# A planner that takes the results of TensorE to be visible later after the end of a step

## Chip, cores and metric

The kernel runs on one core of a Trainium2 chip. The metric is the device time of one execution in microseconds (us). Time before: 4647.31 us, the median of three runs (4646.46 to 4648.82).

## The reference, cut to what matters

The input x holds 32 images of 96 channels and 56 x 56 pixels in f32. Two layers follow each other.

```python
# layer 0: inverted bottleneck, 96 -> 576 -> 96
h = relu(bn(einsum('oc,bchw->bohw', w1, x)))
h = relu(bn(depthwise3x3(h, wdw)))
x = x + bn(einsum('oc,bchw->bohw', w2, h))
# layer 1: tokens t (32, 3136, 96)
t = to_tokens(x)
h = relu(bn(ln(t) @ w1.T))                       # 96 -> 192
X = fft(h, axis=1, norm='ortho')                 # over the 3136 tokens
xr = relu(X.real * rd - X.imag * id + rb)
xi = relu(X.imag * rd + X.real * id + ib)
t = t + bn(ifft(xr + 1j * xi).real @ w2.T)       # 192 -> 96
t = t + ffn(ln(t))      # 96 -> 384 -> 96, operands rounded to fp8 (5,2), sums to f16
```

## The kernel before, in words

Each image passes through four groups of steps, and several images are under way at once.

- **Units** (`unit`, 8 an image: two strips of 28 rows times four blocks of 128 hidden channels). TensorE (PE) expands 96 channels to 128 (L615), ScalarE (ACT) evicts the PSUM result with bias and relu (L625), and the depthwise 3x3 taps are shared out: one on ACT into `acc` (L641), one or two on ACT into `product` (L657), which the GpSimd queue adds to `acc` by an accumulating DMA (L676), and the other six or seven on VectorE (DVE, L668). ACT ends with a relu (L685). The last 64 channels (`last_channels`) go through PE alone (L717, L753), evicted by ACT (L736, L740, L782).
- **front** (one a strip, with `mixer_in`, two a strip). PE projects the hidden channels back in a chain of seven steps (L881, L897, L915) in the PSUM tile `pw`; ACT evicts (L928); DVE takes the layer norm (L825 to L854, with a root on ACT, L835) and scales (L974). PE transposes (L982), projects to 192 (L1000), and does the first stage of the Fourier transform (L1031); ACT evicts each (L985, L1013, L1037). The result goes through DRAM.
- **mid** (two an image). PE does the second Fourier stage (L1118), ACT and DVE apply the diagonal weights and the relus (L1130 to L1165), PE projects 192 to 96 (L1204, L1216; eviction L1230) and inverts the first stage (L1243 to L1247; eviction L1258). Again through DRAM.
- **back** (four an image). PE finishes the inverse (L1324), DVE adds it to the residual (L1329) and takes the norm; ACT quantizes (L1345); PE transposes (L1357; eviction L1361) and computes the feed-forward layer (L1378, L1423) with ACT and DVE in between (L1390, L1396, L1405, L1432, L1435); PE sums up (L1442, L1453), ACT evicts (L1458) and SyncE stores. For the last three images the quantizing goes to DVE.

**What sets the order.** No instruction's place is written by hand. The code above only registers *steps* with the class `Plan`: each has an engine, a planned cost in us, the steps that it comes after, the buffers that it takes at its start and gives back at its end, and a rank. `Plan.emit` then plays the program through once in planned time, while the program is being built: whenever an engine is idle it takes the ready step of the lowest rank whose buffers are free, emits its instructions, and counts the engine as busy for the planned cost. The order in which steps are taken becomes the order of each engine's queue. [...]the planned times have no further effect.

A step's followers become ready, and its buffers free, not at its planned end but a time `late` after it: `Plan.LATE` gives this for PE, ACT and DVE, 0.1 us for the others, and transfers have a rule of their own (`moved`). It applies to every follower, so also to a PE step that comes after another PE step. For PE there are two more rules. [...] And where PE has nothing ready although steps are left,[...] the planner emits a *filler* (L1486), a matmul whose result is not used, to keep the clock up, and counts it as 0.23 us.

Buffers that PE shares with others: three PSUM pairs of banks (`ps`), taken by nearly every PE step or chain and given back by the ACT or DVE step that reads the result; `pw`, one; the SBUF tiles `hs` (3), `acc` (7), `z` (2), `V` (2), `eo` (3), `xnT`, `ya`, `xt`, `u8`, `uT`, `h8` (1 each) and others. A PE step cost is planned by `pe(n, m, passes)`, an ACT step by `act`, a DVE step by `dve`:

```python
def pe(n, m, passes):
    return passes * max(0.855 * n, 0.88 * m) / 1000
```

The line numbers in the profile are those of the program below.

Of the kernel before, what the change touches and what calls it, by code (L numbers as in the profile page):

```python
# [153 lines left out]
class Plan:  # L154
# [5 lines left out]

    LATE = {"PE": 0.23, "ACT": 0.18, "DVE": 0.15}
    WINDOW = 3.413
    LITTLE, FULL = 0.58, 0.965

# [46 lines left out]
    def step(self, engine, cost, emit, after=(), take=(), give=(), late=None, rank=None):  # L213
        late = self.LATE.get(engine, 0.1) if late is None else late
        if rank is None:
            rank = self.now
            self.now += self.pace
        s = Step(engine, cost, emit, list(after), list(take), list(give), late, rank, len(self.steps))
        self.steps.append(s)
        return s  # L220
# [1333 lines left out]
```

## Time and profile before

The span of the profiled execution is 4642.4 us, its mean granted TensorE clock 0.994 of full speed.

| stretch, us | PE busy | DVE busy | ACT busy | granted clock |
|---|---|---|---|---|
| 0 to 150 | 118.20 | 113.23 | 73.72 | 0.85 |
| 150 to 600 | 426.07 | 424.50 | 360.30 | 0.98 to 1.00 |
| 600 to 4200 (3600) | 3537.34 | 3449.78 | 3369.36 | 1.00 |
| 4200 to 4500 (300) | 287.51 | 249.82 | 246.12 | 0.99 to 1.00 |
| 4500 to 4642 | 126.92 | 97.96 | 71.67 | 1.00 |

Two things help in reading the profile of this kernel. Busy time of PE counts matmuls whose ends are modelled, each 0.16 us beyond the start of the next one in a dense stream, so short holes between PE steps don't show as idle time. And a line of the waits names an instruction, the one that released it, the total idle time of the engine just before such instructions, how often, and the longest; it is a wait at the head of a queue[...].

The largest groups are the taps on DVE (L668: 1664 of 1793 ns, 2972.6 us), the expansion (L615) and the projection (L881) on PE (805.3 and 792.8 us), and the product on ACT (L657: 384 of 1588 ns, 609.4 us).

### The profile page before, as it was taken

How to read it: one execution, taken by the hardware profiler on the slowest of the kernel's cores; microseconds unless marked ns; L12 is line 12 of the kernel's file. 1: busy time of each engine (PE TensorE's matmuls, PEld its weight loads, DVE VectorE, ACT ScalarE, POOL GpSimd, SP SyncE). 2: the span in 40 equal slices, each digit the busy share in tenths (PEclk: the TensorE clock that was granted, in tenths of full speed). 3: DMA queues.
4: the chain of work that ended last, by engine and by line, in shares of the span. 5: the costliest groups of instructions: out<-in, count | busy, mean ns of one | idle time of the engine just before them, and what ended most of it. 6: DMA issues, size and time to landing. Idle time of an engine off the chain costs nothing.

```text
span 4642.4 us, 89413 instructions
## 1 busy us (share of the span) xinstructions
PE 4496.0 (97%) x35608; PEld 3351.9 (72%) x35608; DVE 4335.3 (93%) x7053; ACT 4121.2 (89%) x5390; POOL 339.9 (7%) x397
## 2 busy tenths in 40 slices
PE   7999999999999999999999999999999999999998
PEld 4667777777777777777777777777777777777777
DVE  7899999999999999999999999999999999999956
ACT  4677999999999999999999999999999999999854
POOL 0100000000000000000000000000000000000000
PEclk8999999999999999999999999999999999999999
DMA  3577877767877777777767877767776867877753
GB/s 78 130 160 174 192 168 179 183 166 181 187 170 171 187 168 179 185 174 171 184 165 181 187 169 171 187 167 180 187 172 171 187 165 179 191 170 171 170 148 100
DMA packets 390902, 789.51 MB, mean 170 GB/s; under 512 B 135600, under 2 KB 236532, under 8 KB 390484
## 3 DMA queue, kind: packets, MB, share of 16 engines
q1 hardware_dynamic: 335028, 479.15, 37.0%
q0 software_dynamic: 55296, 304.64, 34.1%
q8 instruction: 280, 4.59, 0.4%
q14 instruction: 138, 1.13, 0.1%
q10 hardware_dynamic: 160, 0.01, 0.0%
HBM read 286.38 MB, written 192.68 MB: 103 GB/s over the span
## 4 chain that ended last, share of the span: by engine, by line
PE 56%; ACT 14%; DVE 14%; DMA 5%; issue 3%; SPq 0%; DVEq 0%; ACTq 0%; POOLq 0%
PE pw L881 14%; PE ps L615 9%; DVE acc L668 7%; PE ps L1118 4%; PE ps L1031 3%; PE ps L1000 3%; PE ps L1324 3%; ACT product L657 3%; DMA acc<-product 3%; PE ps L1216 2%; PE ps L753 2%; PE ps L1378 2%; PE pw L915 2%; PE ps L1423 2%; PE ps L717 1%
## 5 line engine op out<-in xcount | busy, mean ns | idle before, releaser
L668 DVE SCALAR_TENSOR_TENSOR acc<-hs,wdw,acc 128x1540 f32<-128x1540 f32 (+2 forms) x1664 | 2972.6, 1793 | 30.1 <-ACT acc L641 22.1
L615 PE MATMUL ps<-xs,w1T 96*128 96x406 f32 x2048 | 805.3, 515 | 18.7 <-ACT hs L625 13.7
L881 PEld LDWEIGHTS pw<-w2T,acc 128*112 128x112 f32 x7168 | 749.4, 178 | 63.6 <-issue 44.5
L881 PE MATMUL pw<-w2T,acc 128*112 128x96 f32 x7168 | 792.8, 264 | 0.5 <-ACT acc L685 0.5
L657 ACT ACTIVATE product<-hs,wdw 128x1568 f32<-128x1568 f32 (+1 forms) x384 | 609.4, 1588 | 17.8 <-DMA product<-product 17.4
L625 ACT ACTIVATE hs<-ps,b 128x812 f32<-128x812 f32 x512 | 478.7, 935 | 114.9 <-PE ps L615 85.1
L615 PEld LDWEIGHTS ps<-xs,w1T 96*128 96x128 f32 x2048 | 363.1, 191 | 251.2 <-issue 177.4
L676 POOL DMA_DIRECT2D acc<-product x256 | 224.6, 877 | 3317.1 <-DVE rf L854 936.7
L641 ACT ACTIVATE acc<-hs,bd,wdw 128x1568 f32<-128x1568 f32 x256 | 435.4, 1701 | 0.2
L685 ACT ACTIVATE acc<-acc 128x1568 f32<-128x1568 f32 x256 | 387.5, 1514 | 42.8 <-DMA acc<-product 42.6
L753 PE MATMUL ps<-hl,band 128*64 128x385 f32 (+3 forms) x3072 | 416.0, 495 | 0.2 <-ACT gc L1258 0.2
L1000 PE MATMUL ps<-watt,xnT 97*120 97x192 f32 x1792 | 334.1, 330 | 16.7 <-DVE V L1147 13.4
L1000 PEld LDWEIGHTS ps<-watt,xnT 97*120 97x120 f32 x1792 | 292.5, 183 | 71.9 <-issue 35.8
L1118 PEld LDWEIGHTS ps<-wb,yb 112*128 112x128 f32 x3528 | 296.6, 165 | 52.2 <-issue 16.0
L1390 ACT ACTIVATE h<-ps 128x784 f16<-128x784 f32 x384 | 315.5, 824 | 15.4 <-PE ps L1378 10.1
L1405 ACT ACTIVATE h<-h 128x784 fp8e5<-128x784 f16 x348 | 298.8, 859 | 34.0 <-DVE h L1396 33.7
L1118 PE MATMUL ps<-wb,yb 112*128 112x112 f32 x3528 | 321.2, 270 | 5.8 <-ACT h L1390 2.5
L1345 ACT ACTIVATE u<-tt,mf,rf 112x96 fp8e5<-112x96 f32 x812 | 315.2, 463 | 0.6 <-DVE mf L857 0.6
L753 PEld LDWEIGHTS ps<-hl,band 128*64 128x64 f32 (+1 forms) x3072 | 152.2, 134 | 209.9 <-issue 180.0
L1486 PE MATMUL pw<-ident 128*128 128x128 f32 x1862 | 268.2, 283 | 3.4 <-ACT xt L928 3.4
L1486 PEld LDWEIGHTS pw<-ident 128*128 128x128 f32 x1862 | 247.4, 197 | 24.9 <-issue 12.5
L1396 DVE TENSOR_SCALAR h<-h,b1q 128x784 f16<-128x784 f16 x384 | 160.2, 418 | 83.9 <-ACT h L1390 81.9
(170 smaller groups left out, 6788.0 us busy)
## 6 DMA issues: line engine op xcount, KB each, us to landing
acc<-product POOLq DMA_DIRECT2D x256, 784.0 KB, 7.3
product<-product POOLq DMA_DIRECT2D x128, 756.0 KB, 10.6
yb<-ydr SPq DMA_DIRECT2D x252, 294.0 KB
wd<-in_wd_dram SPq DMA_DIRECT2D x128, 349.1 KB
wb<-in_wb_dram SPq DMA_DIRECT2D x63, 686.0 KB
ydr<-ya SPq DMA_DIRECT2D x256, 168.0 KB
xs<-in_x_dram SPq DMA_DIRECT2D x64, 609.0 KB
tdr<-xt SPq DMA_DIRECT2D x64, 588.0 KB
```

What stands on the lines that cost most here:

```text
L615: nc.tensor.matmul(u[h][:, j, 0:QW], lhsT=w1T[:, 128 * k : 128 * (k + 1)], rhs=xs[img, s][0:C, at : at + QW], start=True, stop=True,)
L625: nc.scalar.activation(flat[:, 2 * h * QW : 2 * (h + 1) * QW].rearrange("p (j w) -> p j w", j=2), u[h][:, :, 0:QW], AF.Relu, bias=b1[:, k ...
L641: nc.scalar.activation(acc[img, s, k], u["hs"][:, o + up : o + up + R, :], AF.Identity, scale=weight(up, 0), bias=bd[:, k : k + 1],)
L657: nc.scalar.activation(u["p", dr][:, ra:rb, :], u["hs"][:, ra + o + dr : rb + o + dr, :], AF.Copy, scale=weight(dr, 0))
L668: nc.vector.scalar_tensor_tensor(dst, src, weight(dr, dc), dst, ALU.mult, ALU.add)
L685: nc.scalar.activation(acc[img, s, k], acc[img, s, k], AF.Relu)
L753: nc.tensor.matmul(pv[:, :, ca:cb], lhsT=band[rows, j, dc + 1, 64 * o : 64 * o + 64], rhs=H[rows, q : q + 7, ca + dc : cb + dc], skip_grou ...
L881: nc.tensor.matmul(u["pw"][0:SK, t, n % 4, 0:C], lhsT=src[rows, (G * t + n) * SK : (G * t + n + 1) * SK], rhs=rhs, skip_group_check=True, **k,
L1000: nc.tensor.matmul(pv[0:PK, q - a, 0:HA], lhsT=xnT[:, q, 0:PK], rhs=watt, start=True, stop=True,)
L1118: nc.tensor.matmul(o, lhsT=lhsT, rhs=u["wb"][:, G * s + q, :], start=True, stop=True)
L1390: nc.scalar.activation(u["h", c].rearrange("p (j w) -> p j w", j=2), u["H", c][:, :, 0:n], AF.Copy)
L1486: nc.tensor.matmul(pw[:, 0, 4 * C :], lhsT=ident, rhs=ident, start=False, stop=False, skip_group_check=True)
```

## The change

One constant of the planner: the time after the planned end of a PE step at which its followers count as ready and its buffers as free.

```diff
-    LATE = {"PE": 0.23, "ACT": 0.18, "DVE": 0.15}
+    LATE = {"PE": 0.4, "ACT": 0.18, "DVE": 0.15}
```

It is meant to keep ACT and DVE from standing at the head of their queues for a PE result that isn't there yet: in planned time a consumer that becomes ready later finds its engine already given to other ready work, and so it is queued behind that. The arithmetic, the tiles, the buffers and the costs are those of before.

## The prediction

> **What bounds the kernel now.** I read the page first. Its first part gives busy time by engine:
>
> ```profile
> PE 4496.0 (97%) x35608; PEld 3351.9 (72%) x35608; DVE 4335.3 (93%) x7053; ACT 4121.2 (89%) x5390; POOL 339.9 (7%) x397
> ```
>
> Three engines are nearly full at once. Then I took the busy time by stretches, three of them in the middle, each about one image long (columns: stretch, length, busy time of PE, PEld, DVE, ACT, POOL, granted clock, DMA share, GB/s):
>
> ```profile
> 1200.00:1338.50 138.50, 135.64 (x1088) 100.95 (x1086) 132.41 (x211) 129.65 (x172) 11.34 (x13) 1.00 0.74 175
> 1338.50:1477.00 138.50, 136.34 (x1088) 100.86 (x1087) 132.99 (x217) 129.39 (x174) 9.10 (x11) 1.00 0.74 179
> 1477.00:1615.50 138.50, 135.61 (x1083) 100.53 (x1081) 132.25 (x207) 129.36 (x172) 11.96 (x14) 1.00 0.74 173
> ```
>
> Between 600 and 4200 us L668 ran 1347 times; at 52 a image (1664 over 32) that is 25.9 images, so 139 us an image. Of these PE is busy for 136, DVE for 132.5, ACT for 129.5. No engine bounds alone: what the total hangs on is how well one order fits three streams, and 32 x 139 = 4448 us of the 4647 lie in this repetition. The same stretches for the filler line alone show that the order repeats every two images, to the instruction (one filler is two records):
>
> ```profile
> 1200.00:1339.00 139.00, 6.45 (x44) 5.74 (x44) 1.00 0.74 175
> 1339.00:1478.00 139.00, 3.94 (x24) 3.51 (x24) 1.00 0.74 179
> 1478.00:1617.00 139.00, 6.45 (x44) 5.74 (x44) 1.00 0.74 174
> 1617.00:1756.00 139.00, 3.94 (x24) 3.50 (x24) 1.00 0.75 180
> ```
>
> So the planner has settled into a cycle. A changed constant makes it settle into another, and whatever that costs or saves is paid some 30 times. Next, who waits, in the waits between 600 and 4200 us, first DVE's, then ACT's, then PE's (total, times, longest):
>
> ```profile
> DVE tt L1329 <- PE ps L1324: 52.7, 82, 1.7
> DVE h L1396 <- ACT h L1390: 47.3, 42, 2.9
> ACT hs L625 <- PE ps L615: 43.3, 104, 0.8
> ACT al L782 <- PE ps L753: 36.3, 29, 1.3
> ACT z L1013 <- PE ps L1000: 19.6, 24, 1.2
> ACT y L1432 <- PE ps L1423: 16.6, 16, 1.7
> PE ps L1442 <- DVE V L1147: 13.0, 24, 0.9
> PE ps L1423 <- ACT xnT L985: 11.7, 11, 1.1
> ```
>
> Waits on PE cost DVE 52.7/26 = 2.0 us an image; all of ACT's added up are 164 us, 6.3 an image; PE's own are 62.7 us, 2.4 an image. Last, what LATE claims against what the trace has, in the timeline (start, length, engine, line, idle time before):
>
> ```profile
> 2036.47 1.63 PE L615 MATMUL ps<-xs,w1T 96*128 96x406 f32 x4 [0.24 <-ACT h L1390]
> 2037.94 0.73 PE L1246 MATMUL ps<-pj,wc 112*112 112x336 f32 x2
> 2038.14 0.94 ACT L625 ACTIVATE hs<-ps,b 128x812 f32<-128x812 f32 x1 [0.18 <-PE ps L615]
> ```
>
> PE was free for its next step at 2037.94; ACT, which had been idle, started on the result at 2038.14, 0.20 us later. The planner's cost for this step is 4 x 0.855 x 406 = 1.39 us; from 2036.47 to 2038.14 are 1.67, so counted from the planned end the result was late by 0.28. For L1324 the planned cost is 1.38 and DVE started 1.56 after it (0.18). 0.23 lies between the two; 0.40 lies above both.
>
> [...]ACT started 0.04 us after the modelled end (2038.10). [...]the modelled end lies 0.16 us behind the next matmul's start (2038.10 against 2037.94)[...]
>
> **The change, part by part.** No instruction of the real work is added or removed: same matmuls, activations, vector operations, transfers. What moves is the order, and the number of fillers (L1486).
>
> *Consumers on ACT and DVE.* Each PE result is taken to be visible 0.17 us later. An ACT item lasts 129.5/172 = 0.75 us on average. If ACT is backlogged, the chance that it comes free in just those 0.17 us, and so takes something else first, is 0.17/0.75 = 0.23. PE results that ACT reads, from the counts of the groups over 32 images: 16 (L625), 2 + 2 (L736, L782), 4 + 4 (L928, L985), 8 + 8 (L1013, L1037), 6 (L1130), 4 + 4 (L1230, L1258), 4 + 12 + 4 + 4 (L1361, L1390, L1432, L1458) = 82 an image. So about 19 evictions an image go behind one more item, 19 x 0.75 = 14 us of bank time out of 3 x 139 = 417 for the three PSUM pairs: 3.4% more. Queued behind them are the PE steps that want a bank, and then their consumers. ACT itself loses nothing by the swap. What PE loses is bounded by 0 (the bank was spare) and by a doubling of its visible 2.4 us. I take 0.5 us an image, a fifth, since bank use rises by a few per cent[...].
>
> *PE steps behind PE steps.* LATE also holds back a PE step that follows another one, where the two stand in one queue anyway: 16 second expansions, 4 strips, 12 of L881's steps, 4 projections, 3 inversions, 8 of L1378's = 47 hops an image. In the plan each opens a hole of 0.40 instead of 0.23 unless another step is ready. 47 x 0.17 = 8 us if there never is one; by the planner's own costs PE's steps come to some 126 us an image, so PE is in want of work for at most 1 - 126/139 = 9% of the time: 0.7 us, or three more fillers of 0.23. The lower bound is 0. I take 0.3. The holes themselves are only in planned time.
>
> *Buffers given back by PE* (acc, xnT, eo, xt, hl, uT) come free 0.17 later in the plan. A unit takes 139/8 = 17.4 us, so this is 1% of one; I take 0, as DVE's taps (93 of its 132.5 us) are there to be done instead.
>
> *Start and end.* In the first 600 and last 290 us the queues are short[...]. I take 0, within 5 us either way.
>
> Sum: 0.5 + 0.3 = 0.8 us an image, x 32 = 26 us: 4647 + 26 = 4673.
>
> **The rivals.** *Faster.* The waits of ACT and DVE on PE are real, and the planner pays for being early: PE's steps overrun their planned costs (1.47 to the next step for L615 against 1.39), and a margin of 0.17 covers that. DVE's wait for L1324 recurs at 82 of 104 adds, median 0.62 us, so a tap of 1.79 us put ahead of the add would fill it. For: the waits are large and repeat. Against: most are longer than 0.17, so the shift reaches only those whose tie it flips; and PE has just 2.4 idle and 17 x 0.23 = 3.9 of fillers to give. All of DVE's 2.0 us would give 32 x 2.0 = 65, 4582; half, which I take for this case, 4615.
>
> *Much slower.* The new cycle fits worse: PE's bank waits double (2.4) and all three fillers come (0.7): 3.1 x 32 = 99 us, 4746. For: three engines above 93% and single buffers (pw, xnT, ya, real). Against: DVE still has 6.5 idle us an image to absorb some of it.
>
> *No change.* Swaps cancel, the cycle keeps its length: 4647, within 9 us. For: every item is done anyway. Against: a cycle that repeats 30 times makes 0.3 us an image visible.
>
> **How the numbers follow.** Slower by a little 0.42, much slower 0.10, no change 0.10, faster 0.38. The likeliest is 4673. The range goes from 4590, which leaves out the best part of the faster case, to 4740, just short of the much slower one. That gives faster 0.38, within 0.2% 0.10, slower 0.52.
>
> **What would show it.** If I am right: the distance between images rises from 139 to about 140 us; PE's waits on ACT and DVE go above 2.4 us an image; fillers go up from 34 records an image; ACT's waits on PE shrink below 6.3 us, since its consumers come later, without gain. Wrong: if DVE's wait L1329 for L1324 vanishes and DVE's busy share in the middle rises above 96%, the faster case holds. A cycle of another length with the same waits would mean that my sums miss what sets it.

## The result, and the profile after

The changed kernel takes 4614.56 us (median of 4 runs, 4606.50 to 4620.45) against 4648.07 us for the kernel before (also 4 runs, 4646.46 to 4651.47). The ratio is 0.9926, 95% interval 0.9909 to 0.9943: faster by 0.74%, 33.5 us. The forecast was 4673 and slower; the time lies in the stated range, on the other side of the kernel before. It falls on the 4615 of the rival "faster", which had a chance of 0.38; the experiments will show that this agreement is luck.

The first part of the page of the kernel after, busy time by engine:

```profile
PE 4466.9 (97%) x35088; PEld 3312.8 (72%) x35088; DVE 4331.9 (94%) x7053; ACT 4105.6 (89%) x5390; POOL 335.7 (7%) x397
```

ACT and DVE run exactly as many instructions as before (5390 and 7053). PE runs 520 fewer, all of them L1486: fillers, which fell from 1862 records to 1342. In the middle the repetition is another one. The same view of the filler line as before, in stretches of about one image:

```profile
1200.00:1338.20 138.20, 2.56 (x16) 2.21 (x16) 1.00 0.77 178
1338.20:1476.40 138.20, 2.72 (x16) 2.35 (x16) 1.00 0.75 181
1476.40:1614.60 138.20, 2.56 (x16) 2.21 (x16) 0.99 0.75 171
1614.60:1752.80 138.20, 2.72 (x16) 2.35 (x16) 1.00 0.75 180
```

16 records an image take the place of 44 and 24 in turn. In the traces of both kernels ACT and DVE ran their instructions in the order in which the program has them (by line, 5390 of 5390 on ACT and 7053 of 7053 on DVE). ACT's queue shows the cycle itself: in the trace of the kernel after, every instruction of ACT between 1000 and 4100 us stands on the same line of the program as the one 344 places, or two images, earlier. The granted clock of the whole span is 0.987 instead of 0.994.

L668 ran 1356 times between 600 and 4200 us instead of 1347, that is 26.1 images instead of 25.9, or 138.1 us an image instead of 139.0. The two profiled spans differ by 29 us (4642.4 and 4613.1). Followed by the same tap of L668, the kernel after is 0.9 us behind at 600 us (602.2 against 601.4) and 20.6 us ahead at 4200 (4180.6 against 4201.2), so 21 of the 29 us are gained in the middle. The rest comes after that, most of it after the last tap (4389.8 against 4411.5 us).

Lines of the waits between 600 and 4200 us in the kernel after, DVE's, then ACT's, then PE's (total, times, longest):

```profile
DVE tt L1329 <- PE ps L1324: 24.8, 42, 1.2
DVE y L1435 <- ACT y L1432: 16.9, 28, 0.7
DVE h L1396 <- ACT h L1390: 14.9, 33, 3.1
DVE rf L851 <- ACT sdf L835: 14.0, 12, 2.4
...
ACT al L782 <- PE ps L753: 48.5, 42, 1.3
ACT xt L928 <- PE pw L915: 25.6, 38, 1.2
...
ACT hs L625 <- PE ps L615: 21.2, 63, 0.6
...
PE ps L1000 <- DVE V L1147: 34.5, 26, 2.1
```

Two lines of the kernel before that the prediction doesn't show:

```profile
ACT xt L928 <- PE pw L915: 3.9, 13, 1.5
PE ps L1000 <- DVE V L1147: 9.9, 14, 0.9
```

DVE's wait for L1324 has halved (52.7 to 24.8, 82 to 42 times) and so has ACT's for L615 (43.3 to 21.2), as the change intends. But ACT's wait for L753 has risen from 36.3 to 48.5 and its wait for L915 from 3.9 to 25.6; all of ACT's waits on PE together are 6.6 us an image, against 6.3 before. PE's wait at L1000 for DVE's L1147 has grown from 9.9 to 34.5 us. DVE's idle time as a whole fell by 0.8 us an image (5.8 to 5.0), which is the gain as seen from DVE; PE's idle time rose from 2.4 to 2.7 us an image.

The latency itself is what it was, 0.20 us in the step that was measured. In the timeline of the kernel after, a step of L615, the next PE step, and the reader, which found ACT idle:

```profile
2091.07 1.63 PE L615 MATMUL ps<-xs,w1T 96*128 96x406 f32 x4
2092.54 0.49 PE L1378 MATMUL ps<-uT,w1q 96*128 96x392 fp8e5 x2
2092.74 0.94 ACT L625 ACTIVATE hs<-ps,b 128x812 f32<-128x812 f32 x1 [0.19 <-PE ps L615]
```

From 2092.54 to 2092.74 are the 0.20 us of before, and from 2091.07 the 1.67. So 0.40 describes the readers that were measured worse than 0.23 does, and yet the kernel is faster. The experiments ask why.

### The profile page after: what moved, and what is told of

Its sections match the earlier page's. It is cut to its first block, busy times and chain, and to the rows that moved or that the text cites. A ratio compares the mean times of both kernels' runs of the same rounds, so it can differ in the third digit from the quotient of the medians.

```text
span 4613.1 us, 88517 instructions
## 1 busy us (share of the span) xinstructions
PE 4466.9 (97%) x35088; PEld 3312.8 (72%) x35088; DVE 4331.9 (94%) x7053; ACT 4105.6 (89%) x5390; POOL 335.7 (7%) x397
## 4 chain that ended last, share of the span: by engine, by line
PE 66%; DVE 14%; ACT 9%; DMA 8%; issue 3%; SPq 0%; DVEq 0%; POOLq 0%; POOL 0%; ACTq 0%
PE pw L881 17%; PE ps L615 11%; DVE acc L668 7%; PE ps L1000 5%; PE ps L1031 4%; PE ps L1118 4%; DMA acc<-product 4%; PE ps L1324 3%; PE ps L753 3%; PE pw L915 2%; PE ps L717 2%; PE ps L1378 2%; DMA tt<-tdr 2%; PE ps L1423 2%; ACT product L657 2%
## 5 line engine op out<-in xcount | busy, mean ns | idle before, releaser
L668 DVE SCALAR_TENSOR_TENSOR acc<-hs,wdw,acc 128x1540 f32<-128x1540 f32 (+2 forms) x1664 | 2969.7, 1792 | 31.8 <-ACT acc L641 25.6
L615 PE MATMUL ps<-xs,w1T 96*128 96x406 f32 x2048 | 820.8, 524 | 24.1 <-ACT hs L625 16.3
L615 PEld LDWEIGHTS ps<-xs,w1T 96*128 96x128 f32 x2048 | 369.8, 194 | 263.9 <-issue 179.6
L753 PE MATMUL ps<-hl,band 128*64 128x385 f32 (+3 forms) x3072 | 416.6, 495 | 0.0
L1000 PE MATMUL ps<-watt,xnT 97*120 97x192 f32 x1792 | 342.1, 334 | 42.0 <-DVE V L1147 38.3
L1000 PEld LDWEIGHTS ps<-watt,xnT 97*120 97x120 f32 x1792 | 298.5, 186 | 95.7 <-issue 40.3
L1118 PEld LDWEIGHTS ps<-wb,yb 112*128 112x128 f32 x3528 | 296.6, 164 | 55.6 <-issue 15.9
L1390 ACT ACTIVATE h<-ps 128x784 f16<-128x784 f32 x384 | 317.5, 829 | 12.3 <-PE ps L1378 8.8
L1118 PE MATMUL ps<-wb,yb 112*128 112x112 f32 x3528 | 319.6, 270 | 2.8 <-ACT ya L1037 0.9
L753 PEld LDWEIGHTS ps<-hl,band 128*64 128x64 f32 (+1 forms) x3072 | 151.7, 134 | 200.2 <-issue 165.5
L1031 PE MATMUL ps<-z,wa 56*56 56x384 f32 (+1 forms) x2048 | 224.9, 498 | 4.3 <-ACT hs L625 2.8
L1147 DVE SCALAR_TENSOR_TENSOR sb<-ps,cw,V 128x784 f32<-128x784 f32 x192 | 197.1, 1027 | 32.7 <-ACT V L1131 24.6
L1013 ACT ACTIVATE z<-ps 120x768 f32<-120x768 f32 (+1 forms) x256 | 183.6, 725 | 42.3 <-PE ps L1000 41.7
## 6 DMA issues: line engine op xcount, KB each, us to landing
product<-product POOLq DMA_DIRECT2D x128, 756.0 KB, 10.2
```

The costliest lines, as they stand in the source:

```text
L615: nc.tensor.matmul(u[h][:, j, 0:QW], lhsT=w1T[:, 128 * k : 128 * (k + 1)], rhs=xs[img, s][0:C, at : at + QW], start=True, stop=True,)
L668: nc.vector.scalar_tensor_tensor(dst, src, weight(dr, dc), dst, ALU.mult, ALU.add)
L753: nc.tensor.matmul(pv[:, :, ca:cb], lhsT=band[rows, j, dc + 1, 64 * o : 64 * o + 64], rhs=H[rows, q : q + 7, ca + dc : cb + dc], skip_grou ...
L1000: nc.tensor.matmul(pv[0:PK, q - a, 0:HA], lhsT=xnT[:, q, 0:PK], rhs=watt, start=True, stop=True,)
L1031: nc.tensor.matmul(u["y", b][64 * c : 64 * c + n, j, 0 : 2 * HA], lhsT=wa[at, 0:n], rhs=rhs, start=True, stop=True)
L1118: nc.tensor.matmul(o, lhsT=lhsT, rhs=u["wb"][:, G * s + q, :], start=True, stop=True)
```

## The experiments

The theories, with the letters that the expectations use. **A**, margin: consumers further back in the queues wait less, and this is the gain. **B**, another cycle: the planner falls into a different repeating order, and its length has little to do with where the consumers were meant to go. **C**: the gain is the fillers that went away. **D**: the nearer LATE is to the measured latency, the better. **E**, formed after twelve runs: a draw, but with a tendency in favour of a large LATE. Each experiment starts from the kernel before.

### One or two nanoseconds

For 0.229 and 0.402 the planner writes other orders than for 0.23 and 0.40.

```diff
-    LATE = {"PE": 0.23, "ACT": 0.18, "DVE": 0.15}
+    LATE = {"PE": 0.229, "ACT": 0.18, "DVE": 0.15}   # second kernel: 0.402
```

> LATE for PE is 0.229 in place of 0.23, one nanosecond less. Theory A (margin: the change helped because consumers are queued later, so they wait less for PE): nothing to speak of, 4648 within 9 us, and 34 filler records an image as before. Theory B (another cycle: 0.23 happens to lead the planner into a repeating order that is worse than its neighbours', and any value that leaves it gains): as large a move as the change's, 4605 to 4630, with another repeating order and clearly fewer fillers than 34 records an image.

> LATE for PE is 0.402, two nanoseconds more than in the changed kernel. Theory A (margin): 4615 within 9 us, like the changed kernel. Theory B (another cycle): a different repeating order, off by some tens of us from 4615, and as easily slower than before: 4650 to 4700.

0.229 gives 4603.82 us, ratio 0.9910 (0.9896 to 0.9925): one nanosecond less gains at least as much as 0.17 us more. 0.402 gives 4670.01 us, 1.0055 (1.0040 to 1.0070): slower than before, and 55 us behind 0.40. Theory A, as an account of the gain, is refuted by both. The traces of 0.23 and 0.229 show where the orders part. The queues of PE (fillers aside), ACT and DVE hold the same work in the same order until about 750 us. There PE takes the same steps up to L1378 and L615 in both, and then another one, first with 0.23, then with 0.229:

```profile
748.34 1.53 PE L615 MATMUL ps<-xs,w1T 96*128 96x406 f32 x4
749.70 1.46 PE L1000 MATMUL ps<-watt,xnT 97*120 97x192 f32 x8
```

```profile
752.55 1.53 PE L615 MATMUL ps<-xs,w1T 96*128 96x406 f32 x4
753.92 1.72 PE L881 MATMUL pw<-w2T,acc 128*112 128x96 f32 x16
```

One step is taken ahead of another, and every later choice is made in another state: of ACT's 4703 instructions from there on, 2626 places hold an instruction of another line. B had forecast the large move and fewer fillers: they fell to 25 records an image, and the time lies 1 us below B's range. DVE's longest waits with 0.229, and with 0.402, both between 600 and 4200 us:

```profile
DVE h L1396 <- ACT h L1390: 50.2, 72, 3.3
DVE tt L1329 <- PE ps L1324: 28.3, 58, 0.8
DVE eo L1162 <- ACT V L1153: 11.0, 26, 0.6
```

```profile
DVE h L1396 <- ACT h L1390: 47.7, 49, 3.1
DVE sta L825 <- ACT xt L928: 32.4, 24, 3.1
DVE tt L1329 <- PE ps L1324: 23.5, 53, 1.2
DVE eo L1162 <- ACT V L1153: 22.8, 52, 0.9
```

The wait that the prediction watched, L1329 for L1324, is halved in both, in the faster kernel and in the slower one. What grew with 0.402 are waits on ACT: those for L928 and L1153 are 55 us here, against 19.8 before.

### The order of before without its fillers

```diff
-                    self.filler()
+                    if not 600 < now < 4100:
+                        self.filler()
```

> The kernel before, where the planner still counts its fillers but emits none between 600 and 4100 us of planned time; the real work stands in the order of before. Only matmuls whose result nobody uses are left out. Theory C (the gain is the fillers that went away, 17 to 8 an image, each 0.23 us of a bound PE): taking away all 17 in 25 images gives 25 x 17 x 0.23 = 98 us, so about 4550. If fillers only fill holes that the order has anyway: 4648 within 15 us; if the clock falls for want of them, slower, with a mean granted clock below 0.98.

4674.77 us, 1.0063 (1.0048 to 1.0078): slower. The page of this kernel has PE at 4481.5 us busy, nearly the 4496.0 of before, with 858 fewer records; the mean granted clock is 0.979. Its largest PE waits between 600 and 4200 us:

```profile
PE ps L1000 <- DVE V L1147: 34.2, 26, 1.6
PE ps L1378 <- ACT ya L1037: 22.9, 11, 2.1
PE ps L1442 <- DVE V L1147: 17.4, 24, 1.1
```

In the trace, ACT, DVE and, fillers aside, PE run line for line the order of before. PE is idle for 4.5 us an image instead of 2.4, and some of its matmuls take longer (L1324 276 ns in the mean instead of 263, L1118 277 instead of 270). Theory C falls in its simple form: in the order of before, taking the fillers out costs 30 us (4645.18 for the kernel before beside it). They sit in holes of that order, and without them the mean granted clock was 0.979 instead of 0.994. That the changed kernel does with half of them at 0.987 goes with fewer holes: PE's idle and filler time together are 7.5 us an image before and 5.4 after.

### LATE taken apart

LATE for PE does three things: it holds back readers on other engines, PE steps behind PE steps, and buffers. Three events in place of one let each be set alone; with 0.23 for all three the program is that of before, with 0.40 for all three that of after.

```diff
+    READ, SAME, GIVE = 0.4, 0.23, 0.23   # second kernel: SAME alone 0.4; third: GIVE alone
...
-                    heapq.heappush(events, (now + cost + late, count + 1, None, s))
...
+                        parts = ((self.READ, "read"), (self.SAME, "same"), (self.GIVE, "give"))
...
+                    for n, (l, what) in enumerate(parts):
+                        heapq.heappush(events, (now + cost + l, count + 1 + n, None, (s, what)))
```

> The planner's PE lateness is split in three, and only the part that holds back the readers on ACT and DVE is 0.40; PE steps behind PE steps and the buffers that PE gives back stay at 0.23. Theory A (margin for the consumers): this is the part that the change was made for, so 4615 within 15 us. Theory B (another cycle): a draw of its own, anywhere from 4600 to 4690, with no reason to agree with the changed kernel.

> Only the part that holds back a PE step behind another PE step is 0.40, the readers on ACT and DVE and the buffers stay at 0.23. Theory A: no gain, as no consumer moves back: 4648, or slower by the 0.3 us an image of the prediction's filler term (4658). Theory B: a draw of its own, and as nearly every draw beats 0.23's cycle, more likely 4600 to 4640.

> Only the part that holds back the buffers which PE steps give back is 0.40. Theory A, and the prediction's step on these buffers: 4648 within 9 us. Theory B: this too leads the planner elsewhere; a draw of its own, 4600 to 4690.

Readers alone: 4696.80 us, 1.0100 (1.0085 to 1.0115). PE behind PE alone: 4633.54, 0.9965 (0.9951 to 0.9979). Buffers alone: 4643.78, 0.9991 (0.9984 to 0.9998). The part that the change was made for loses 49 us on its own, 7 us beyond the range that B had given; the other two gain 14 and 4. Added up, the three would lose 31 us; set together, as in the changed kernel, they gain 33.5. The parts do not add, which theory A and the prediction's sum both need. Buffers alone are no draw of their own, against B: in the trace ACT's queue differs from that of before in 197 of 5390 places only (after the change, in 2810), so the planner came back to the cycle of before. With the readers alone the planner doesn't settle: of ACT's order between 1000 and 4100 us, no more than 65% comes again at any distance of up to six images. DVE's waits when only the readers are held back:

```profile
DVE h L1396 <- ACT h L1390: 46.2, 57, 6.0
DVE y L1435 <- ACT y L1432: 36.3, 20, 5.0
DVE acc L668 <- ACT acc L641: 22.2, 41, 1.3
...
DVE tt L1329 <- PE ps L1324: 10.2, 22, 1.2
```

DVE hardly waits for PE any more (10.2 us instead of 52.7), but longer for what ACT makes of PE's results: waits of up to 6.0 us for L1390 and 36.3 us in total for L1432.

### A constant that has nothing to do with TensorE, and all three together

```diff
-    LATE = {"PE": 0.23, "ACT": 0.18, "DVE": 0.15}
+    LATE = {"PE": 0.23, "ACT": 0.181, "DVE": 0.15}   # second kernel: 0.239, 0.185, 0.141
```

> PE's lateness stays at 0.23; ACT's goes from 0.18 to 0.181, one nanosecond, a constant that has nothing to do with TensorE's results. Theory A: 4648 within 9 us. Theory B: another cycle, 4600 to 4640, and other filler counts than 34 records an image.

> All three latenesses moved a little together: PE 0.239, ACT 0.185, DVE 0.141. Theory B: a draw near 0.23's neighbours, 4600 to 4650, with a fair chance to beat both kernels (below 4606). Theory D: PE's is further from 0.20 than before, so not below 4648.

4662.67 us, 1.0029 (1.0021 to 1.0036), and 4675.27 us, 1.0053 (1.0038 to 1.0068). The first moves by more than theory A allows it. Neither lies where B had put it: I had assumed that nearly every other order beats that of 0.23, and here are two that lose to it.

### The value of LATE, from 0.10 to 0.50

Each of these kernels changes the same constant to the value in its name.

> LATE for PE is 0.10, less than the 0.2 us that the trace shows from a free PE to the start of a consumer. Theory A (margin): consumers come too early, the waits of ACT and DVE on PE grow above before's 6.3 and 2.0 us an image, and the time is above 4660. Theory B (another cycle): a draw of its own, more likely better than 0.23's: 4590 to 4640.

> LATE for PE is 0.22, close to the measured 0.20 us and 9 ns from 0.229. Theory B (every value a draw, most draws better than 0.23's): 4600 to 4640, DVE's waits on PE nearer 28 us than 53 us between 600 and 4200 us. Theory D (no draw but a trend: the nearer to the measured latency, the better): 4604 or less, at or below the run with 0.229.

> LATE for PE is 0.38. Theory B: a draw; from the changed kernel's 4615 nothing follows, 4600 to 4690. Theory A in a weaker form (around 0.4 the margin helps, and 0.402 was the accident): 4615 within 9 us.

> LATE for PE is 0.50, more than twice the measured latency. The prediction's mechanism (consumers too late, banks held longer, 0.8 us an image for 0.17 us) would give 0.27/0.17 x 26 = 41 us over before: 4690. Theory B: a draw between 4600 and 4700. Theory A without a limit: below 4615.

The next six were fixed together beforehand, three below and three above, to tell a tendency from a mere draw:

> LATE for PE is 0.21. Only a draw: no side is favoured, 4600 to 4700. A tendency (theory E: the plan drifts less from the chip when PE's results are taken to be later): with 0.24 and 0.25 the mean is 4640 to 4665, above before or near it.

> LATE for PE is 0.24. Only a draw: 4600 to 4700. Theory E: with 0.21 and 0.25 a mean of 4640 to 4665.

> LATE for PE is 0.25. Only a draw: 4600 to 4700. Theory E (a tendency): with 0.21 and 0.24 a mean of 4640 to 4665.

> LATE for PE is 0.36. Only a draw: 4600 to 4700. Theory E: with 0.44 and 0.48 the mean is 4610 to 4635, 20 us or more below that of 0.21, 0.24 and 0.25, and DVE's waits on ACT are below 5 us an image.

> LATE for PE is 0.44. Only a draw: 4600 to 4700. Theory E: with 0.36 and 0.48 a mean of 4610 to 4635.

> LATE for PE is 0.48. Only a draw: 4600 to 4700. Theory E: with 0.36 and 0.44 a mean of 4610 to 4635.

All values of PE's LATE that were run. The waits are those above 0.15 us between 600 and 4200 us in the trace, divided by the images in that stretch (L668's count over 52).

| LATE, us | time, us | against before | DVE waits for ACT, us an image | DVE for PE | ACT for PE |
|---|---|---|---|---|---|
| 0.10 | 4647.06 | 1.0004 (0.9995 to 1.0013) | 5.3 | 0.6 | 6.8 |
| 0.21 | 4668.91 | 1.0047 (1.0032 to 1.0062) | 7.1 | 0.3 | 7.0 |
| 0.22 | 4665.74 | 1.0044 (1.0027 to 1.0061) | 6.1 | 0.5 | 6.4 |
| 0.229 | 4603.82 | 0.9910 (0.9896 to 0.9925) | 3.5 | 1.1 | 6.5 |
| 0.23 (before) | 4648.07 | 1 | 3.4 | 2.0 | 6.3 |
| 0.24 | 4621.46 | 0.9940 (0.9925 to 0.9955) | 4.2 | 0.9 | 6.7 |
| 0.25 | 4676.34 | 1.0067 (1.0050 to 1.0084) | 6.1 | 0.6 | 6.6 |
| 0.36 | 4638.94 | 0.9977 (0.9970 to 0.9984) | 5.1 | 0.5 | 6.1 |
| 0.38 | 4608.80 | 0.9921 (0.9902 to 0.9941) | 3.9 | 0.8 | 5.7 |
| 0.40 (after) | 4614.56 | 0.9926 (0.9909 to 0.9943) | 3.6 | 1.0 | 6.6 |
| 0.402 | 4670.01 | 1.0055 (1.0040 to 1.0070) | 5.9 | 0.9 | 8.7 |
| 0.44 | 4689.00 | 1.0085 (1.0068 to 1.0101) | 6.5 | 0.7 | 6.6 |
| 0.48 | 4726.35 | 1.0167 (1.0146 to 1.0188) | 8.1 | 1.3 | 6.7 |
| 0.50 | 4616.58 | 0.9933 (0.9918 to 0.9948) | 4.5 | 0.1 | 5.5 |

Of the 13 values other than 0.23, six are faster than before, six slower, and one the same. B's guess that most values beat 0.23 is missed by 0.10 and by 0.22, and 0.48 lies 26 us above the range that was given for any draw. Theory A would have 0.10 above 4660, and it is no slower than before. A's weaker form, that a margin around 0.4 helps, has 0.38 on its side, and falls with 0.36 and 0.44. Theory D falls with 0.22, which is 62 us slower than 0.229. Theory E falls with the six: 0.21, 0.24 and 0.25 have a mean of 4656 us, 0.36, 0.44 and 0.48 one of 4685, the reverse of what it says. Over all values, the six from 0.21 to 0.25 have a mean of 4647 us and the seven from 0.36 to 0.50 one of 4652, while single values scatter with a standard deviation of 35 us. No slope can be seen in that, neither the gain of theory A nor the 26 us of loss for 0.17 us that the prediction had worked out (0.50 was to be 41 us slower and is 31 us faster). With six and seven values the difference of the two means has a standard error of about 20 us, so a tendency of up to some 40 us between the groups stays open.

The columns say where a bad order loses. DVE's waits for PE, which the change aims at, don't go with the time: they are lowest at 0.50, which is among the quickest, and at 0.21, which is among the slow, and highest before. ACT's waits for PE vary little, but for 0.402. DVE's waits for ACT do go with it among these values: 3.5 to 4.5 us in all kernels below 4625 us, 5.9 to 8.1 in all above 4660. But this is no rule: the kernel with ACT's lateness at 0.181 takes 4662.67 us with 4.3 us of waits for ACT and 1.9 for PE. DVE's waits at 0.50 and at 0.48:

```profile
DVE h L1396 <- ACT h L1390: 32.8, 48, 1.1
DVE acc L668 <- ACT acc L641: 28.9, 27, 1.2
DVE eo L1162 <- ACT V L1153: 25.7, 51, 0.7
DVE rf L851 <- ACT sdf L835: 18.6, 46, 1.7
...
DVE tt L1329 <- PE ps L1324: 1.1, 2, 0.5
```

```profile
DVE rf L851 <- ACT sdf L835: 77.3, 40, 3.3
DVE eo L1162 <- ACT V L1153: 75.0, 65, 3.7
DVE tt L1329 <- PE ps L1324: 31.6, 50, 1.5
DVE h L1396 <- ACT h L1390: 30.1, 40, 1.5
```

At 0.48 the two waits of 77.3 and 75.0 us are for a root (L835, 0.21 us in the median in the kernel before) and a relu (L1153, 0.85 us), each of which takes far less than the longest wait for it (3.3 and 3.7 us); what they stood behind in ACT's queue is not shown. As DVE's own work is the same wherever it was worked out (3449.8/25.9 = 133 us an image before, 3468.9/26.1 = 133 after, 3427.1/25.7 = 133 without the fillers), its idle time is the image time by another name; so this shows where the loss falls. Why a given value leads to a given order, and why one order is shorter than another, stays open. The kernel before is the odd one in the table: few waits for ACT and the most for PE, those ahead of L1329.

The planner's own forecast doesn't tell the good orders from the bad either. The planned time at which `Plan.emit` ends (`now` at its end, when the program is built) is 4526 us for the kernel before and 4508 for the changed one, the right way round, but 4504 for 0.48, the slowest of all, and 4535 for 0.50, one of the quickest. Over the 19 different orders its correlation with the measured time is 0.33.

## Why the prediction was wrong

**Wrong: the sign, by the step "Consumers on ACT and DVE".** It took a chance of 0.23 for each eviction to go behind one more item, 14 us of bank time, and priced that at 0.5 us an image of loss for PE. The step that failed is this pricing: it lays the postponement on top of an order that otherwise stays, while the runs show that it makes another order. PE's idle time did go up, from 2.4 to 2.7 us an image, less than the 0.5, while DVE's fell by 0.8, for which the step had no term. ACT's waits for PE, which were to shrink, rose from 6.3 to 6.6. Readers held back alone lose 49 us, not 16 (0.5 x 32), and with the two other parts they gain. The 0.5 itself, a fifth of PE's 2.4, had no measurement behind it.

**Wrong: the fillers.** Up to three more an image were forecast, from the 47 hops of PE behind PE; there came nine fewer (34 records on average to 16), and that part of the change alone gained 14 us. Also wrong is the rival's view of fillers as PE time that could be had back: without them the order of before is 30 us slower.

**Right: the buffers**, priced at nothing: alone they give 4643.78, within 0.1%, in nearly the order of before. Right as well: the latency of 0.20 us, which the kernel after shows again. What it was worth for the time was not: no run shows that a value near it is better.

**Wrong: the end**, put at nothing within 5 us. After the last tap of L668 the lead of the kernel after grows from 21.7 to 29.3 us. What it does better there stays open. Two readings were a little off, without weight in the sum: the 62.7 us given as PE's waits are its whole idle time (the waits are 61.4), and DVE's idle time is 5.8 us an image, not 6.5.

**Right, and not followed: the cycle.** The first part of the prediction says that the planner had settled into a cycle, that a changed constant makes it settle into another, and that the difference is paid some 30 times. The forecast that follows from this is a wide one, centred on the time before: equal chances for both sides and little for no change. The runs give it: six faster, six slower, one the same, with a scatter of 35 us. In the traces these are cycles of different lengths: ACT's order comes again after two images with 0.40, after three with 0.38 and 0.402. Instead the sum moved the centre by 26 us, less than that scatter, on the strength of a latency whose weight the runs don't show. The range of 4590 to 4740, drawn from the rivals, holds all 13 other values.

**The rival "faster"** named a wait that did shrink: L1329's for L1324 was to be halved, 2.0 to 1.0 us an image, and it went to 0.95, and DVE's busy share in the middle rose from 95.8 to 96.4%, as the prediction's sign for this case has it. Its reason, a margin for overruns, does not hold: 0.229, with less margin, halves the wait too, and 0.402, with more, halves it and is slower. So that the time came to its 4615 is luck.

## What to carry to other kernels

Where a greedy planner writes the order, and three engines are over 93% busy in the middle, a changed constant mostly draws a new order, and its result says little about the constant: try its neighbours first, a nanosecond to either side, to learn the scatter, and believe a tendency only beyond it. By the same token the scatter is a resource: many nearby values can be tried and the best order kept, by measured time and not by planned time (0.229 has the lowest here, 0.9910 of before against 0.9926; the intervals overlap). And look for the loss where the waits go to, not only at the wait that the edit removes: here most of the slow orders wait longer for ACT, the engine between PE and DVE.

## What the runs showed of the hardware that was not expected

Discarded matmuls in the holes of PE's queue were worth 0.63%: with the same order of the real work and 858 fewer matmul records, the mean granted clock went from 0.994 to 0.979 and the time from 4645 to 4675 us. PE was busy for nearly as long (4481.5 us instead of 4496.0), as some of the matmuls that remained took longer (L1324 276 ns in the mean instead of 263).
